# A Mamba layer's scans: the product for the next group issued mid-group, softplus in small steps, and two jobs of later layers moved beside the scans

## The chip, the cores and the metric

The kernel runs on one core of a Trainium2 chip. Its engines are TensorE (PE, with its weight loads as PEld), VectorE (DVE), ScalarE (ACT), GpSimd (POOL) and SyncE (SP), which issues most transfers here. Each engine works through its own queue in order, and semaphores tie the queues together. The metric is the time of one execution on the device in microseconds (us); the lower, the better.

## What is computed

A network of four layers on x of 2 images, 256 channels, 48 x 48 positions (2304 tokens per image), all in float32. Layer 0 is a bidirectional Mamba layer, layer 1 a linear attention with a depthwise convolution and an MLP after a group norm, layer 2 an attention and a mixture of experts that is routed over a graph, layer 3 an attention and a second mixture of experts. What the change touches, cut from the reference:

```python
# layer 0, for each direction s in (f, b)
xs = silu(conv4(xi) + conv_b)                      # 512 inner channels
proj = xs @ xproj_w.T                              # 16 for dt, 16 for B, 16 for C
dt = softplus(proj[..., :16] @ dtproj_w.T + dtproj_b)
def step(h, ...):                                  # h: 512 channels x 16 states
    h = exp(d_t[..., None] * A) * h + (d_t * u_t)[..., None] * B_t[:, None, :]
    return h, einsum('bdn,bn->bd', h, C_t)         # u is xs
y = ys + u * D;  out = seq + ((y_f + y_b) * silu(z)) @ out_proj_w.T

# layer 1 begins with a group norm: 32 groups of 8 channels, one mean and variance
# per group and image over all positions
# layer 2, three heads: e = x @ W_embed[h].T + b_embed[h]; q, k, v are thirds of the
# sequence; the output goes through W_out. The kernel multiplies W_embed[h].T with
# itself and with W_out.T beforehand, so that only 256 x 512 is needed per head.
```

## The kernel before

**Order of the queues.** The kernel is written with a framework that takes the instructions in the order in which the Python code emits them, assigns buffers and semaphores, and then makes each engine's queue itself: an instruction that is ready early in its planning can stand ahead of one that was emitted before it. The order in the code is thus a priority; the order on the chip is read from the trace.

**Layer 0.** Tokens are cut into chunks of W = 384 columns, NCH = 6 per image. `order` lists 24 chunks: image 0 forward, image 0 backward, image 1 forward, image 1 backward. `scan` works through one chunk: 4 blocks of 128 channels (d) times 16 states (n) make 64 scans of 128 x 384, taken in 16 groups of GN = 4 states. A group needs
- `bb` and `cc` (L354, L356): 4 rows each of B and C, broadcast to 128 partitions by a transfer on SP, used by two groups, two buffers each;
- `db` (L359): POOL's product of `dtu` (dt times u) and `bb`, 128 x 1536, two buffers;
- for each state: ACT's exp into PSUM (`hs`, L376, five banks), DVE's scan (L382 forward, L385 backward), the product with C (`hc`, L390: on POOL where `on_pool`, for one or two states of a group, else on DVE), a copy of the last column into `state` (L392, ACT), and a matmul with the identity that adds `hc` into `yp` (L344).

After every second state, a slot, `scan` lets the generators in `beside` go on, in proportion: 32 slots in a chunk. One is `prepare` (L252) for the next chunk, 15 steps by slot 25: convolution on PE, Silu, the projection to dt, B and C, then softplus as max(v, 0) + log(1 + exp(-|v|)) with a correction for the rounding of 1 + exp(-|v|): exp (L302), 1 + exp (L305), log (L307), minus 1 (L308), all on ACT; L310, L311 and L312 on DVE over 128 x 1536; the product `dtu` on POOL (L314). Another is `project_in` (L168), layer norm and input projection of a later chunk, in the first ten chunks; a third `project_out` (L318), which adds a finished backward chunk to the residual `xres` (L328). Outside of `scan`, PSUM results go through one bank (`hold`, tag mm).

**Layer 1** begins with `group_norm(0)` (L510): twelve `bn_stats` on DVE (L517), two tiny matmuls with `gmat`, and the normalization (L533) into `xn`; then L547 multiplies with the weights. Lists of edges for layer 2 are sorted on DVE meanwhile (`sort_list`, `sort_rest`).

**Layer 2** begins with the products of its weights for three heads: loads of `w_eo` (L708, L709), 72 matmuls L713 and 144 matmuls L721 of one column; then transposes (L741) and the first product of the attention, L750, which needs `gm`.

Of the kernel before, what the change touches and what calls it, by code (L numbers as in the profile page):

```python
# [18 lines left out]
F32 = mybir.dt.float32  # L19
# [33 lines left out]
class Env:  # L53
# [20 lines left out]

    def uid(self):
        self.n_pools += 1
        return self.n_pools
# [41 lines left out]

def load_x(E, b, c):  # L120
    xin = E.p["x"].rearrange("b (k p) n -> p b k n", p=P)
    E.nc.sync.dma_start(
        E.xres[:, :, b * L + c * W : b * L + (c + 1) * W], xin[:, b, :, c * W : (c + 1) * W]
    )
# [4 lines left out]
def layer0(ctx, E):  # L129

# [32 lines left out]
    def hold():  # L163

        pool, tag = (ps, "mm") if scanning else (psh, "hs")
        return pool.tile([P, W], F32, tag=tag, name="mm")

    def project_in(b, c):  # L168
# [15 lines left out]
        rs = up.tile([P, W], F32, tag="rs", name="rs")  # L184
# [6 lines left out]
        nc.vector.reciprocal(rs, rs)  # L191
        yield
        nc.vector.tensor_tensor(h, h, bc(rs, [P, 2, W], 1), ALU.mult)
        for k in range(2):
            nc.vector.scalar_tensor_tensor(
                h[:, k, :], h[:, k, :], E.v("ln_g", k, 1), pos[:, k, :], ALU.mult, ALU.add
            )
        yield
# [39 lines left out]
    one = big.tile([P, 2], F32, name="one")  # L238
    nc.vector.memset(one[:, 0:1], 1.0)
    nc.vector.memset(one[:, 1:2], -1.0)  # L240
# [11 lines left out]
    def prepare(b, s, c, got):  # L252
# [52 lines left out]
        nc.scalar.activation(dtu, ex, AF.Identity, bias=one[:, 0:1])  # L305
        yield
        nc.scalar.activation(ln, dtu, AF.Ln)  # L307
        nc.scalar.activation(dtu, dtu, AF.Identity, bias=one[:, 1:2])  # L308
        yield
        nc.vector.tensor_tensor(ex, ex, dtu, ALU.subtract)  # L310
        nc.vector.tensor_tensor(dt, dt, ln, ALU.add)  # L311
        nc.vector.tensor_tensor(dt, dt, ex, ALU.add)  # L312
        yield
        nc.gpsimd.tensor_tensor(dtu, dt, xs, ALU.mult)  # L314
        got.extend((b, s, c, xs, y, dt, dtu, bcd))
        yield
# [14 lines left out]
    def scan(step, beside, b, s, c, xs, y, dt, dtu, bcd):  # L331
# [20 lines left out]
        for d0, g in [(d0, g) for d0 in range(0, DB, 2) for g in range(NS // GN)]:  # L352
            bb = wp.tile([P, GN, W], F32, tag="bb", name="bb")
            nc.sync.dma_start(bb, bcd[16 + g * GN : 16 + (g + 1) * GN, :].partition_broadcast(P))  # L354
            cc = wp.tile([P, GN, W], F32, tag="cc", name="cc")
            nc.sync.dma_start(cc, bcd[32 + g * GN : 32 + (g + 1) * GN, :].partition_broadcast(P))  # L356
            for d in (d0, d0 + 1):
                db = wp.tile([P, GN, W], F32, tag="db", name="db")
                nc.gpsimd.tensor_tensor(db, bc(dtu[:, d, :], [P, GN, W], 1), bb, ALU.mult)  # L359
                if g == 0:  # L360

                    while waiting and waiting[0][1] < d0:
                        add_state(*waiting.pop(0)[1:])
                    yp[d] = psy.tile([P, W], F32, tag=f"y{d % 2}", name=f"yp{d}")
                    nc.tensor.matmul(
                        yp[d], lhsT=w_d[s][:, d, :], rhs=xs[:, d, :], start=True, stop=False
                    )
                    if not fwd:
                        nc.tensor.matmul(
                            yp[d], lhsT=E.ident, rhs=yf[:, d, :], start=False, stop=False  # L370
                        )
                for j in range(GN):
                    n = g * GN + j
                    on_pool = j in GP[(g + d) % 2]
                    hs = psh.tile([P, W], F32, tag="hs", name="hs")
                    nc.scalar.activation(  # L376
                        hs, dt[:, d, :], AF.Exp, scale=nega[s][:, d * NS + n : d * NS + n + 1]
                    )
                    to = wp.tile([P, W], F32, tag="ho", name="ho", bufs=4) if on_pool else hs
                    init = 0.0 if step == 0 else state[:, d, n : n + 1]  # L380
                    if fwd:
                        nc.vector.tensor_tensor_scan(to, hs, db[:, j], init, ALU.mult, ALU.add)  # L382
                        last = to[:, W - 1 : W]
                    else:
                        nc.vector.tensor_tensor_scan(  # L385
                            to[:, ::-1], hs[:, ::-1], db[:, j, ::-1], init, ALU.mult, ALU.add
                        )
                        last = to[:, 0:1]
                    hc = wp.tile([P, W], F32, tag="hcp" if on_pool else "hc", name="hc", bufs=4)
                    (nc.gpsimd if on_pool else nc.vector).tensor_tensor(hc, to, cc[:, j, :], ALU.mult)  # L390
                    if step < NCH - 1:
                        nc.scalar.copy(state[:, d, n : n + 1], last)  # L392
                    while waiting and waiting[0][0] + LAG <= at:
                        add_state(*waiting.pop(0)[1:])
                    if on_pool:
                        waiting.append((at, d, hc))
                    else:
                        add_state(d, hc)
                    at += 1
                    if j % 2:  # L400
                        slot += 1
                        for i, (steps, n_steps, end) in enumerate(beside):
                            while done[i] * end < n_steps * slot and next(steps, beside) is not beside:
                                done[i] += 1
# [4 lines left out]
        for steps, _, _ in beside:  # L409
            for _ in steps:  # L410
                pass

# [7 lines left out]
    for _ in prepare(0, "f", 0, ready):  # L420
        pass
    scanning = True
    pieces = [(0, c) for c in range(2, NCH)] + [(1, c) for c in range(NCH)]
    after = None
    for i, (b, s, step, c) in enumerate(order):
        now, ready = ready, []
        beside = [(after, 2, 5)] if after else []
        if i + 1 < len(order):
            nb, s2, _, c2 = order[i + 1]
            beside.append((prepare(nb, s2, c2, ready), 15, 25))  # L430
        if i < len(pieces):
            beside.append((project_in(*pieces[i]), 12, 32))
        scan(step, beside, *now)
# [26 lines left out]
def layer1(ctx, E, edges):  # L460
# [21 lines left out]
    gmat = big.tile([P, P], F32, name="gmat")  # L482
    same_block(E, lw, gmat, 3, 1.0 / 8)
# [26 lines left out]
    def group_norm(b):  # L510

        xb = E.xres[:, :, b * L : (b + 1) * L]
        mv = wp.tile([P, 2, 2], F32, tag="mv", name="mv")
        for k in range(2):
            st = wp.tile([P, NCH, 6], F32, tag="st", name="st")
            for c in range(NCH):
                nc.vector.bn_stats(st[:, c, :], xb[:, k, c * W : (c + 1) * W])  # L517
            nc.vector.bn_aggr(mv[:, k, :], st)
        pg = ps.tile([P, 2], F32, tag="mm", name="pg")
        nc.tensor.matmul(pg, lhsT=gmat, rhs=mv[:, :, 0], start=True, stop=True)  # L520
        gm = wp.tile([P, 2], F32, tag="gm", name="gm")
        nc.vector.tensor_copy(gm, pg)
        dv = wp.tile([P, 2], F32, tag="dv", name="dv")
        nc.vector.tensor_tensor(dv, mv[:, :, 0], gm, ALU.subtract)
        nc.vector.tensor_tensor(dv, dv, dv, ALU.mult)
        nc.vector.tensor_tensor(dv, dv, mv[:, :, 1], ALU.add)
        gv = ps.tile([P, 2], F32, tag="mm", name="gv")
        nc.tensor.matmul(gv, lhsT=gmat, rhs=dv, start=True, stop=True)
        gr = wp.tile([P, 2], F32, tag="gr", name="gr")
        nc.scalar.activation(gr, gv, AF.Sqrt, bias=E.eps[1e-5])  # L530
        nc.vector.reciprocal(gr, gr)
        for k in range(2):
            nc.vector.tensor_scalar(  # L533
                E.xn[:, k, b * L : (b + 1) * L], xb[:, k, :], gm[:, k : k + 1], gr[:, k : k + 1],
                ALU.subtract, ALU.mult,
# [151 lines left out]
def layer2_attn(ctx, E):  # L687
# [3 lines left out]

    nc, tc, p = E.nc, E.tc, E.p
    NH, D = 3, 768
    S = L // NH
    DT, ST, HW2 = D // P, S // P, S // 2
# [4 lines left out]
    ub = big.tile([P, NH, 4], F32, name="ub")  # L700
    with (
        tc.tile_pool(name="l2wt", bufs=2) as wts,
        tc.tile_pool(name="l2wps", bufs=2, space=PSUM) as ps,
    ):
        for h in range(NH):

            w_eo = wts.tile([P, DT, 2 * C], F32, tag="w_eo", name="w_eo")
            nc.sync.dma_start(w_eo[:, :, 0:C], p["W_embed"][h].rearrange("(k p) m -> p k m", p=P))  # L708
            nc.sync.dma_start(w_eo[:, :, C:], p["W_outT"].rearrange("(k p) m -> p k m", p=P))  # L709
            for m in range(2):  # L710
                pg = ps.tile([P, 2 * C], F32, tag="pg", name="pg")
                for k in range(DT):
                    nc.tensor.matmul(  # L713
                        pg, lhsT=w_eo[:, k, m * P : (m + 1) * P], rhs=w_eo[:, k, :],
# [1230 lines left out]
```

## Time and profile before

| what | value |
|---|---|
| three timed runs | 5452.36, 5459.55, 5462.36 us; median 5459.55 |
| the profiled execution, its own time | 5504.47 us |
| its span | 5502.7 us, 47222 instructions |
| busy, share of the span | PE 87%, PEld 48%, DVE 64%, ACT 43%, POOL 44% |
| mean granted TensorE clock | 0.949 |
| layer 0's scans | 103 to 2391 us |
| layer 2's weight products | 3118 to 3182 us |

The profiled execution is slower than the timed ones by 0.8%; durations come from it. A row of the profile names the engine, the line of kernel.py, the operation, what it writes and reads, the shapes, and in brackets how long the engine had been idle before it and what ended that. A busy share over the whole span mixes stages with different limits, so the stages are read one by one.

### The profile page before, as it was taken

How to read it: one execution, taken by the hardware profiler on the slowest of the kernel's cores; microseconds unless marked ns; L12 is line 12 of the kernel's file. 1: busy time of each engine (PE TensorE's matmuls, PEld its weight loads, DVE VectorE, ACT ScalarE, POOL GpSimd, SP SyncE). 2: the span in 40 equal slices, each digit the busy share in tenths (PEclk: the TensorE clock that was granted, in tenths of full speed). 3: DMA queues.
4: the chain of work that ended last, by engine and by line, in shares of the span. 5: the costliest groups of instructions: out<-in, count | busy, mean ns of one | idle time of the engine just before them, and what ended most of it. 6: DMA issues, size and time to landing. Idle time of an engine off the chain costs nothing. (4 is left out here: it accounts for less than half of the span.)

```text
span 5502.7 us, 47222 instructions
## 1 busy us (share of the span) xinstructions
PE 4797.7 (87%) x15246; PEld 2649.9 (48%) x15246; DVE 3499.6 (64%) x5380; ACT 2371.5 (43%) x4935; POOL 2398.4 (44%) x1295
## 2 busy tenths in 40 slices
PE   7888788888877787879999999998799999998996
PEld 3444344444333343435555555565455555554664
DVE  4899988888999888999994234456534401212333
ACT  5767777666767566622222123322023322222220
POOL 3888887888989888830000000048412100001112
PEclk8999999999999899999999899999899999999997
DMA  4444444443444444421100100111111100001323
GB/s 155 166 171 177 165 178 160 160 157 137 173 150 173 150 161 153 151 100 37 41 26 2 39 1 0 37 38 24 14 58 46 46 6 6 9 6 23 83 76 80
DMA packets 173646, 486.56 MB, mean 88 GB/s; under 512 B 31487, under 2 KB 96516, under 8 KB 173124
## 3 DMA queue, kind: packets, MB, share of 16 engines
q1 hardware_dynamic: 165252, 471.82, 24.3%
q0 software_dynamic: 8128, 11.55, 1.6%
q8 instruction: 124, 2.03, 0.1%
q14 instruction: 142, 1.16, 0.1%
HBM read 416.44 MB, written 66.86 MB: 88 GB/s over the span
## 5 line engine op out<-in xcount | busy, mean ns | idle before, releaser
L344 PE MATMUL yp<-hc,ident 128*128 128x384 f32 x3072 | 1199.9, 523 | 293.7 <-DVE hc L390 253.8
L359 POOL TENSOR_TENSOR db<-dtu,bb 128x1536 f32<-128x1536 f32 x384 | 1333.3, 3473 | 45.5 <-issue 16.5
L344 PEld LDWEIGHTS yp<-hc,ident 128*128 128x128 f32 x3072 | 574.7, 198 | 875.3 <-DVE hc L390 451.3
L390 POOL TENSOR_TENSOR hc<-ho,cc 128x384 f32<-128x384 f32 x576 | 582.6, 1020 | 183.6 <-DVE ho L382 81.9
L390 DVE TENSOR_TENSOR hc<-hs,cc 128x384 f32<-128x384 f32 x960 | 501.3, 544 | 38.9 <-PE yp L344 37.7
L376 ACT ACTIVATE hs<-dt,negab 128x384 f32<-128x384 f32 x768 | 435.2, 582 | 92.6 <-DVE ho L385 41.4
L376 ACT ACTIVATE hs<-dt,negaf 128x384 f32<-128x384 f32 x768 | 434.6, 582 | 58.4 <-DVE hc L390 27.7
L385 DVE TENSOR_TENSOR_SCAN hs<-hs,state,db 128x384 f32<-128x384 f32 x400 | 396.6, 1015 | 55.8 <-POOL db L359 30.3
L382 DVE TENSOR_TENSOR_SCAN hs<-hs,state,db 128x384 f32<-128x384 f32 x400 | 397.1, 1014 | 30.0 <-POOL db L359 23.2
L1770 POOL DMA_INDIRECT xe<-xt_d,token x48 | 52.4, 1091 | 726.4 <-issue 715.0
L266 PE MATMUL mm<-xw,w_cv 128*128 128x384 f32 x768 | 288.8, 512 | 64.5 <-ACT xs L270 26.6
L1704 PE MATMUL po<-at,xtok 128*128 128x384 f32 x864 | 329.7, 506 | 7.7 <-ACT at L1702 7.5
L912 POOL PARTITION_ALL_REDUCE most<-most x1 | 0.4, 382 | 738.8 <-DVE most L911 738.8
L1354 PE MATMUL ph<-xn,w 128*128 128x384 f32 x768 | 292.9, 523 | 28.0 <-issue 10.4
L1695 PE MATMUL sp<-qT,xn 128*128 128x384 f32 x864 | 317.2, 486 | 0.0
L1702 ACT ACTIVATE at<-sp 128x384 f32<-128x384 f32 x216 | 104.9, 491 | 472.5 <-PE sp L1695 472.4
L1358 ACT ACTIVATE hid<-ph,vec 128x384 f32<-128x384 f32 x192 | 110.8, 582 | 338.8 <-PE ph L1354 254.5
L627 PE MATMUL pf<-t,wfc 128*128 128x384 f32 x768 | 255.4, 489 | 0.0
L646 PE MATMUL po<-hid,wfc 128*128 128x384 f32 x768 | 253.6, 486 | 0.0
L385 DVE TENSOR_TENSOR_SCAN ho<-hs,state,db 128x384 f32<-128x384 f32 x240 | 241.2, 1005 | 15.3 <-ACT hs L376 15.1
L382 DVE TENSOR_TENSOR_SCAN ho<-hs,state,db 128x384 f32<-128x384 f32 x240 | 240.3, 1001 | 6.3 <-ACT hs L376 6.2
L266 PEld LDWEIGHTS mm<-xw,w_cv 128*128 128x128 f32 x768 | 146.0, 196 | 192.7 <-ACT xs L270 43.2
(434 smaller groups left out, 7962.9 us busy)
## 6 DMA issues: line engine op xcount, KB each, us to landing
bb<-bcd SPq DMA_DIRECT2D x192, 768.0 KB
cc<-bcd SPq DMA_DIRECT2D x192, 768.0 KB
xw<-xi_d SPq DMA_DIRECT2D x24, 774.0 KB
w<-in_m_w SPq DMA_DIRECT2D x16, 1024.0 KB
y_d<-y SPq DMA_DIRECT2D x32, 384.0 KB
ye<-y_d SPq DMA_DIRECT2D x32, 384.0 KB
xi_d<-xz SPq DMA_DIRECT2D x48, 192.0 KB
z_d<-xz SPq DMA_DIRECT2D x48, 192.0 KB
```

Of the source, the lines that this page charges most:

```text
L266: nc.tensor.matmul(px, lhsT=w_cv[b, s][:, d * 4 + k, :], rhs=xw[:, d, o : o + W], start=k == 0, stop=k == 3,)
L344: nc.tensor.matmul(yp[d], lhsT=E.ident, rhs=hc, start=False, stop=summed[d] == NS)
L359: nc.gpsimd.tensor_tensor(db, bc(dtu[:, d, :], [P, GN, W], 1), bb, ALU.mult)
L376: nc.scalar.activation(hs, dt[:, d, :], AF.Exp, scale=nega[s][:, d * NS + n : d * NS + n + 1])
L382: nc.vector.tensor_tensor_scan(to, hs, db[:, j], init, ALU.mult, ALU.add)
L385: nc.vector.tensor_tensor_scan(to[:, ::-1], hs[:, ::-1], db[:, j, ::-1], init, ALU.mult, ALU.add)
L390: (nc.gpsimd if on_pool else nc.vector).tensor_tensor(hc, to, cc[:, j, :], ALU.mult)
L627: nc.tensor.matmul(pf, lhsT=wfc1[:, k, f * P : (f + 1) * P], rhs=t1[:, k, :], start=k == 0, stop=k == 1,)
L646: nc.tensor.matmul(po[m], lhsT=wfc2[:, f, m * P : (m + 1) * P], rhs=hid[:, i, :], start=f == 0, stop=f == 15,)
L1354: nc.tensor.matmul(ph, lhsT=w1[:, e, k, f * P : (f + 1) * P], rhs=xn[:, k, c * W : (c + 1) * W], start=k == 0, stop=k == 1,)
L1695: nc.tensor.matmul(sp, lhsT=xn[:, k, t0 + i * P : t0 + (i + 1) * P], rhs=qT[:, k, c * W : (c + 1) * W], start=k == 0, stop=k == 1,)
L1704: nc.tensor.matmul(po[m], lhsT=xtok[:, i, m * P : (m + 1) * P], rhs=at, start=i == 0, stop=i == MT - 1,)
```

## The change

- `begin_group` (new) loads `bb` and `cc` where a pair of groups begins and makes `db`. It is called for the next group after the second state of a group (`j == 1`), also for the first group of the next chunk; before, these stood at the head of each group.
- `prepare` has 19 steps by slot 29 instead of 15 by 25. L308 is gone: its minus 1 is folded into a `scalar_tensor_tensor`. After log come two empty steps, then one step per block of 128 channels with three DVE instructions of 384 columns, and `dtu` for that block on POOL a step later.
- `project_in` has its reciprocal and the two products after it by halves, in 14 steps instead of 12.
- `head_products` (new) makes layer 2's weight products beside the scans, in the twelve chunks after the last `project_in`, three steps in each, with half of the inner dimension at a time: loads; three matmuls of 512 columns, which ACT copies for the first half and DVE adds for the second; six matmuls of one column with one or two small DVE instructions. The result goes to DRAM (`gm_d`), and layer 2 loads it in three transfers.
- `group_stats` (new) holds the statistics of `group_norm`. For image 0 it runs beside the second forward chunk of image 1, in 15 steps; for image 1 it runs where it ran.
- PSUM tiles are declared 512 columns wide and used to 384; `gmat` is made at the very start; the normalization of one piece in layer 3 has a pool of its own.

```diff
+def group_stats(E, wp, bank, b):
...
+    for k in range(2):
+        st = wp.tile([P, NCH, 6], F32, tag="st", name="st")
+        for c in range(NCH):
+            nc.vector.bn_stats(st[:, c, :], xb[:, k, c * W : (c + 1) * W])
+            yield
+        nc.vector.bn_aggr(mv[:, k, :], st)
+    pg = bank()
+    nc.tensor.matmul(pg, lhsT=E.gmat, rhs=mv[:, :, 0], start=True, stop=True)
+    nc.vector.tensor_copy(gm, pg)
+    yield
...
     def project_in(b, c):
...
-        nc.vector.reciprocal(rs, rs)
-        yield
-        nc.vector.tensor_tensor(h, h, bc(rs, [P, 2, W], 1), ALU.mult)
         for k in range(2):
+            half = rs[:, k * (W // 2) : (k + 1) * (W // 2)]
+            nc.vector.reciprocal(half, half)
+            yield
+        for k in range(2):
+            nc.vector.tensor_tensor(h[:, k, :], h[:, k, :], rs, ALU.mult)
             nc.vector.scalar_tensor_tensor(
                 h[:, k, :], h[:, k, :], E.v("ln_g", k, 1), pos[:, k, :], ALU.mult, ALU.add
             )
-        yield
+            yield
...
         nc.scalar.activation(ln, dtu, AF.Ln)
-        nc.scalar.activation(dtu, dtu, AF.Identity, bias=one[:, 1:2])
         yield
-        nc.vector.tensor_tensor(ex, ex, dtu, ALU.subtract)
-        nc.vector.tensor_tensor(dt, dt, ln, ALU.add)
-        nc.vector.tensor_tensor(dt, dt, ex, ALU.add)
         yield
-        nc.gpsimd.tensor_tensor(dtu, dt, xs, ALU.mult)
-        got.extend((b, s, c, xs, y, dt, dtu, bcd))
-        yield
+        for d in range(DB + 1):
+            if d:
+                nc.gpsimd.tensor_tensor(
+                    dtu[:, d - 1, :], dt[:, d - 1, :], xs[:, d - 1, :], ALU.mult
+                )
+            if d < DB:
+                nc.vector.scalar_tensor_tensor(
+                    ex[:, d, :], dtu[:, d, :], -1.0, ex[:, d, :], ALU.add, ALU.subtract
+                )
+                nc.vector.tensor_tensor(dt[:, d, :], dt[:, d, :], ln[:, d, :], ALU.add)
+                nc.vector.tensor_tensor(dt[:, d, :], dt[:, d, :], ex[:, d, :], ALU.subtract)
+            else:
+                got.extend((b, s, c, xs, y, dt, dtu, bcd))
+            yield
...
+    def head_products():
+        DT, D = 6, 768
+        for h, m, z in [(h, m, z) for h in range(3) for m in range(2) for z in range(2)]:
+            w_eo = []
+            for k in range(3):
+                rows = slice((z * 3 + k) * P, (z * 3 + k + 1) * P)
+                t = up.tile([P, 2, W], F32, tag=("pos", "h", "sq")[k], name="w_eo")
+                t = t.rearrange("p k w -> p (k w)")[:, : 2 * C]
+                nc.sync.dma_start(t[:, 0:C], p["W_embed"][h, rows, :])
+                nc.sync.dma_start(t[:, C:], p["W_outT"][rows, :])
+                w_eo.append(t)
+            yield
...
+            yield
...
+            yield
+
+    def begin_group(q, b, s, c, xs, y, dt, dtu, bcd):
+        d0, g, d = groups[q]
+        if d == d0:
+            for n, o in (("bb", 16), ("cc", 32)):
+                held[n] = wp.tile([P, GN, W], F32, tag=n, name=n)
+                nc.sync.dma_start(
+                    held[n], bcd[o + g * GN : o + (g + 1) * GN, :].partition_broadcast(P)
+                )
+        db = wp.tile([P, GN, W], F32, tag="db", name="db")
+        nc.gpsimd.tensor_tensor(db, bc(dtu[:, d, :], [P, GN, W], 1), held["bb"], ALU.mult)
+        return db, held["cc"]
...
+                if j == 1:
+                    if q + 1 < len(groups):
+                        begun = begin_group(q + 1, b, s, c, xs, y, dt, dtu, bcd)
+                    elif following:
+                        begun = begin_group(0, *following)
...
-            beside.append((prepare(nb, s2, c2, ready), 15, 25))
+            beside.append((prepare(nb, s2, c2, ready), 19, 29))
         if i < len(pieces):
-            beside.append((project_in(*pieces[i]), 12, 32))
-        scan(step, beside, *now)
+            beside.append((project_in(*pieces[i]), 14, 32))
+        elif i < len(pieces) + 12:
+            beside.append((islice(heads, 3), 3, 32))
+        if (b, s, step) == (1, "f", 1):
+            beside.append((group_stats(E, up, lambda: hold()[:, 0:2], 0), 15, 32))
+        begun = scan(step, beside, begun, ready, *now)
...
+    for h in range(NH):
+        nc.sync.dma_start(gm[:, h], E.gm_d[h].rearrange("m p c -> p m c"))
```

## The prediction

> **What bounds the kernel now.** The execution on the page spans 5502.7 us and took 5504.47; the three timed runs have a median of 5459.55, 0.8% less. I sum against 5504.47 and scale the result by 5459.55/5504.47 = 0.992. No change smaller than 0.2% (11 us) can be told from none. Part 4 of the page covers only the tail of the last layer, so I went by stage: part 2, then a windows table, then waits and timelines of each stretch that the diff touches.
>
> Part 2 of the page, busy tenths in slices of 137.6 us:
> ```profile
> DVE  4899988888999888999994234456534401212333
> ...
> POOL 3888887888989888830000000048412100001112
> ```
> The first seventeen slices are layer 0's scans. DVE and POOL are both near full there and PE has room. The windows table puts numbers on the scans (103 to 2391 us), on the way into layer 1, and on the start of layer 2 (window, length, then busy us of PE, PEld, DVE, ACT, POOL, and the granted clock):
> ```profile
> 103.00:2391.00 2288.00, 1852.43 (x4994) 914.77 (x4994) 2077.37 (x2677) 1554.32 (x3575) 1962.28 (x983) 0.95 0.44 160
> 2399.00:2418.00 19.00, 1.66 (x6) 1.40 (x6) 18.39 (x49) 2.03 (x4) 4.90 (x4) 0.59 0.92 315
> 3118.00:3185.00 67.00, 66.25 (x230) 43.02 (x230) 18.46 (x46) 0.58 (x1) 0.38 (x1) 0.73 0.19 64
> ```
> The scans are 24 chunks of 95.3 us on average; DVE is idle for 211 us of them (8.8 per chunk), POOL for 326. From 3118 to 3185 PE works alone, on layer 2's weight products. What DVE waits for, and the one wait of POOL that matters, 100 to 2392 us (total, times, longest):
> ```profile
> DVE hs L382 <- POOL db L359: 39.4, 35, 6.8
> ...
> DVE hs L385 <- POOL db L359: 35.4, 34, 2.5
> DVE dt L311 <- ACT state L392: 25.0, 13, 3.6
> ...
> DVE dt L311 <- ACT ln L307: 7.0, 5, 3.1
> DVE ex L310 <- ACT dtu L308: 5.1, 8, 1.2
> ```
> ```profile
> POOL dtu L314 <- DVE dt L312: 96.9, 17, 9.9
> ```
> One chunk shows how they hang together (timelines of DVE, then POOL):
> ```profile
> 2184.64 1.76 DVE L311 TENSOR_TENSOR dt<-dt,ln 128x1536 f32<-128x1536 f32 x1 [1.33 <-ACT state L392]
> 2186.31 1.75 DVE L310 TENSOR_TENSOR ex<-ex,dtu 128x1536 f32<-128x1536 f32 x1
> ...
> 2189.15 1.74 DVE L312 TENSOR_TENSOR dt<-dt,ex 128x1536 f32<-128x1536 f32 x1
> ...
> 2198.85 1.93 DVE L385 TENSOR_TENSOR_SCAN hs<-hs,state,db 128x384 f32<-128x384 f32 x2 [2.02 <-POOL db L359]
> ```
> ```profile
> 2191.04 3.44 POOL L314 TENSOR_TENSOR dtu<-dt,xs 128x1536 f32<-128x1536 f32 x1 [7.03 <-DVE dt L312]
> ...
> 2195.38 3.44 POOL L359 TENSOR_TENSOR db<-dtu,bb 128x1536 f32<-128x1536 f32 x1
> ```
> POOL stands 7.03 us at the head of its queue for DVE's softplus; its next db lands late, and the scan waits 2.02 us (and 0.62 at the group after).
>
> **Part 1, db issued at j == 1 of the group before.** POOL's queue already runs a group ahead: at the end of the stage its order is db 2377.93, hc 2381.33, db 2382.28, hc 2385.67, and that last db is for a group whose first scan starts about 2386.3, while the hc after it belongs to the group before. The order out of the program is thus not the order in the queue, and I book nothing for the move itself: same 384 products, same bb and cc loads (two buffers each, issued when a buffer comes free), ahead of the same hc. If it helps where POOL is behind, that is in the next sum.
>
> **Part 2, softplus in small steps.** Per prepared chunk (23 of them inside the scans):
> - *db waits.* The two rows make 74.8 us, of which 12.2 fall in the first chunk, which the change leaves alone: 62.6. In the chunk shown 2.64 of 3.11 come from the 7.03 us stall, 85%. With four dtu products of a quarter width, each issued a step after its dt, the stall should go: -53 (0 to -63).
> - *ACT.* L308 goes (1.58 us). From the exp at 2181.22 to the next scan fed by ACT at 2188.22 DVE did 3.51 us of softplus in a gap that it could not have scanned in. The hole in the exps becomes 6.4 - 1.58 = 4.8 us, but softplus now comes two empty steps later and no longer fills it: 4.8 + 3.5 - 6.4 = +1.9 per chunk at worst (+44), 1.58 less at best (-36). I take the middle, +4.
> - *More instructions.* Three of 1.75 (5.25) become eight TENSOR_TENSOR and four SCALAR_TENSOR_TENSOR of 384 columns. L390 runs in pairs 0.46 apart, L195 0.51: 4 x (0.46 + 0.46 + 0.51) = 5.7, +0.47 per chunk, +11. POOL's 3.43 becomes 4 x 0.97, +0.45, on POOL's own slack (326 us). In project_in one reciprocal of 2.55 becomes two of half the width, one product of 0.95 two of half: nothing within 0.1 each.
> - *Waits between DVE and POOL.* The three instructions read both inputs from SBUF, and such an instruction does not start while POOL works:
> ```profile
> 1523.68 1.92 DVE L310 TENSOR_TENSOR ex<-ex,dtu 128x1536 f32<-128x1536 f32 x1
> ...
> 1525.99 4.51 DVE L312 TENSOR_TENSOR dt<-dt,ex 128x1536 f32<-128x1536 f32 x1
> ```
> ```profile
> 1523.94 4.94 POOL L359 TENSOR_TENSOR db<-dtu,bb 128x1536 f32<-128x1536 f32 x1
> ```
> POOL's db, begun under L310, took 4.94 instead of 3.44, and L312 behind it 4.51 instead of 1.74. Inside the scans L310 to L312 lose 21.6 us over 69 instructions this way, L193 11.8 over 9, L195 0.8 over 22. Today the stall at dtu keeps POOL quiet just when L310 to L312 run; the change takes that cover away and makes four arrivals of one. Ends: no wait (-22), or the 2.77 of the L312 above at every step (4 x 23 x 2.77 - 22 = +233). The first instruction of a step should wait as L310 to L312 and L193 do, (21.6 + 11.8)/78 = 0.43, and the two right behind it as L195, 0.04 each: 0.51 per step. That is 92 x 0.51 - 22 = +25, and +5 for the second step that project_in gets in nine chunks.
>
> The Trainium skill, page "SBUF — State Buffer", section "Who interferes with whom", says that a DVE instruction with two SBUF inputs contends with a GpSimd instruction that reads SBUF, and that whoever issues first holds the shared port for its whole length while the other fully blocks; the 4.51 and 4.94 above agree. Taken alone it speaks against this change: POOL is inside a db 16 x 3.44 of 95.3 us, 58%, so each of twelve instructions would wait 0.58 x 1.72 = 1.0 us, an estimate from that page's rule, and the sum would be 276 - 22 = +254 in place of +25. I go by L195, whose two follow one another directly and hardly wait.
>
> Scans: -53 + 4 + 11 + 30 = -8.
>
> **Part 3, group norm of batch 0.** Before, layer 0's last add ends at 2399.7 and layer 1's first matmul (L547) starts at 2417.61, after twelve bn_stats and two tiny matmuls. After, only the two L533 (1.47 each) remain. POOL's memset of img holds DVE until 2403.8 (a CAST takes 4.24 there), so about 2407: -10.6; layer 1 is then full on DVE (191.5 of 200 us), where at least the 12 x 0.47 removed counts: -9 (-4 to -13).
>
> **Part 4, layer 2's products.** 72 matmuls L713 and 144 L721 leave a PE that has no one beside it. L750 stood at 3185.16. The first 1.57 MB that were loaded there from 3113.23 were used at 3118.3; gm is 1.57 MB, and the transposes L741 need none of it. L750 could start at 3118.5: -66.6. But 18.46 us of DVE work (normalization and sorting, third window) lay under the products and now stand before the copies and maxima of the attention: between -66.6 and -48 I take half, -58.
>
> **What parts 3 and 4 add to the scans.** bn_stats 12 x 0.47 and ten small ones: 7 us on DVE in one chunk. Products: six adds of 128x512 (0.69 for L717), eighteen tiny ones: 6 us over twelve chunks. PE takes 2 to 4 us more per chunk; it waits today for hc, and DVE's four hc buffers hide it. If they do not, another 24. The loads (9.4 MB) lie 16 slices of a chunk ahead, DMA share 0.44; if SP stood behind one, bb and cc would too, and they have a pair of groups in hand. +13 (0 to +37). The rest has one answer, nothing: same_block at the very start lies beside the first loads, the banks of 512 columns are the same banks, and layer 3's separate pool has the same work.
>
> **Sum:** -8 - 9 - 58 + 13 = -62 on 5504.47; x 0.992 = -61.5; 5459.55 - 61.5 = **5398 us**.
>
> **Rivals.**
> *The scans gain what they wait for:* softplus still finds POOL quiet. -63 - 36 + 11 - 11 = -99 for the scans, -153 in all: 5308. For it: a stall of 96.9 us goes. Against: in chunks 13 to 17, where POOL seldom stalls, a chunk takes 86.5 to 91.6 us, and 16 x 3.43 + 24 x 0.97 + 4 x 0.97 + 5.7 = 87.8 is a floor once POOL and those instructions exclude one another.
> *The port wait takes the stall's place (slower):* POOL always has a product in hand, and a step waits as L312 does in chunks 12 to 19 of 0 to 23, 13.4/8 = 1.67. 101 steps x 1.67 - 22 = +147; scans -53 + 4 + 11 + 147 = +109; in all +55: 5514. It decides from (54 + 53 - 4 - 11 + 22)/101 = 1.13 us per step on. For it: that row is of chunks with a busy POOL. Against: 0.31 per instruction over the whole stage.
> *The mid-group issue does nothing and the small steps nothing for db:* POOL goes from waiting for one long dt to waiting for four short ones. db waits 0 instead of -53: -9 in all, 5451.
>
> **How the numbers follow.** Forecast 0.45 (own range 5370 to 5430), faster scans 0.25, port wait 0.15, nothing for db 0.15. Faster by over 0.2%: 0.44 + 0.25 + half of the last 0.07 = 0.76; within 0.2%: 0.08; slower: 0.16. The range leaves out the fast half of the first rival and most of the slow one: 5315 to 5480.
>
> **What would show it.** Right: L713 and L721's successors lie before 2400, the first L750's successor starts within 15 us of the last layer 1 add; the first layer 1 matmul within 9 us of it; POOL's wait for dt under 30 us; the scans' length within 30 of 2288. Wrong: softplus instructions of 384 columns with a mean over 0.9 us (the port), DVE waits for db still at 60, or DVE rows piled up ahead of layer 2's copies.

## The result, and the profile after

The changed kernel took 5515.76 us (median of four runs, 5511.01 to 5521.27) against 5457.56 (5452.36 to 5462.36) of the kernel before, run beside it: ratio 1.0108, 95% interval 1.0096 to 1.012. It is slower by 58 us where 5398 us was forecast. The profiled execution took 5511.01 us, its span is 5509.2.

Part 2 of its page, busy tenths in slices of 137.7 us:
```profile
DVE  5999999999999999999998334446734401212333
...
POOL 3887787778888887882000000018712100001112
```
DVE, which had digits of 8 and 9 in the scans, now has nothing but 9 after the first slice, and for a slice longer. The windows table gives the numbers (scans, the way into layer 1, the start of layer 2; columns as before):
```profile
93.80:2515.60 2421.80, 1952.98 (x5217) 969.12 (x5218) 2280.81 (x2950) 1535.64 (x3562) 1991.99 (x1054) 0.93 0.45 156
2516.00:2531.00 15.00, 7.54 (x21) 3.69 (x20) 13.80 (x24) 1.76 (x3) 5.22 (x3) 0.84 0.53 159
3213.00:3238.00 25.00, 16.19 (x52) 9.17 (x50) 16.82 (x30) 3.87 (x5) 0.00 (x0) 0.83 0.19 63
```
The scans last 2421.8 us instead of 2288.2: +133.6. DVE is busy for 203 us more (2077.4 to 2280.8) and idle for 70 less (211 to 141). The two gaps behind them did shrink: from the last scan to layer 1's first matmul 26.5 to 14.6 us, from layer 1's last matmul (L646, now L738) to the attention's first in layer 2 73.3 to 13.5; in the 25 us that end there DVE now works 16.8 (third row: normalization and sorting, which lay under the products before). The scans also begin 9.1 us earlier. That is 133.6 - 9.1 - 11.9 - 59.7 = +52.9, and +55 with 2.5 that layer 2's attention is longer; +58 was timed. The two profiled executions differ by only 7 us because that of before spent 51 us more in a part that nothing touches, layer 2's experts (846 us from their first matmul to layer 3's first, against 796 here and 799 to 809 in every run below).

What DVE waits for in the scans, and POOL's wait for softplus:
```profile
DVE hc L489 <- PE yp L449: 41.5, 38, 4.3
...
DVE hs L481 <- POOL db L432: 9.9, 17, 1.7
...
DVE hs L484 <- POOL db L432: 7.7, 14, 0.8
```
```profile
POOL dtu L350 <- DVE dt L359: 53.1, 59, 4.3
```
The waits for db are down from 74.8 to 17.6 us, as the change meant; 6.8 of the 74.8 stood before the first scan, so 50 were won between the first scan and the last. The price stands in no list of waits, only in how long instructions take (groups by shape: busy us, mean ns):
```profile
L489 DVE TENSOR_TENSOR hc<-hs,cc 128x384 f32<-128x384 f32 x960 | 501.0, 539 | 43.3 <-PE yp L449 41.5
...
L358 DVE TENSOR_TENSOR dt<-dt,ln 128x384 f32<-128x384 f32 x92 | 128.7, 1403 | 7.0 <-ACT state L491 5.4 <-ACT ln L345 1.5
L359 DVE TENSOR_TENSOR dt<-dt,ex 128x384 f32<-128x384 f32 x94 | 103.6, 1103 | 0.0
L355 DVE SCALAR_TENSOR_TENSOR ex<-dtu,ex 128x384 f32<-128x384 f32 x92 | 90.2, 1003 | 10.9 <-ACT dtu L343 7.7 <-ACT state L491 2.9
L234 DVE SCALAR_TENSOR_TENSOR h<-h,vec,pos 128x384 f32<-128x384 f32 x20 | 33.5, 1680 | 0.0
```
An undisturbed one of L355 to L359 takes 0.53 to 0.55 us. Summing over all 276 what each takes beyond that gives 172 us, 0.62 each; before, 69 wide ones lost 21. In project_in L233 and L234 lose 33 us where 12 were lost. A timeline of DVE, then POOL, shows how:
```profile
1809.60 2.99 DVE L358 TENSOR_TENSOR dt<-dt,ln 128x384 f32<-128x384 f32 x1
1812.52 1.01 DVE L481 TENSOR_TENSOR_SCAN hs<-hs,state,db 128x384 f32<-128x384 f32 x1
1813.44 0.53 DVE L359 TENSOR_TENSOR dt<-dt,ex 128x384 f32<-128x384 f32 x1
...
1815.29 0.52 DVE L355 SCALAR_TENSOR_TENSOR ex<-dtu,ex 128x384 f32<-128x384 f32 x1
1815.73 1.35 DVE L358 TENSOR_TENSOR dt<-dt,ln 128x384 f32<-128x384 f32 x1
1817.01 1.01 DVE L481 TENSOR_TENSOR_SCAN hs<-hs,state,db 128x384 f32<-128x384 f32 x1
1817.93 2.84 DVE L359 TENSOR_TENSOR dt<-dt,ex 128x384 f32<-128x384 f32 x1
```
```profile
1808.75 3.42 POOL L432 TENSOR_TENSOR db<-dtu,bb 128x1536 f32<-128x1536 f32 x1
...
1815.51 1.16 POOL L489 TENSOR_TENSOR hc<-ho,cc 128x384 f32<-128x384 f32 x1 [0.45 <-PE yp L449]
1816.63 3.73 POOL L432 TENSOR_TENSOR db<-dtu,bb 128x1536 f32<-128x1536 f32 x1
```
The L358 at 1809.60 ends 0.42 us after POOL's db, the L359 at 1817.93 0.41 us after the next: each ends only once POOL's instruction has ended. Between them a scan runs at its usual 1.01 us and an hc at 0.54. The second thing to see is the order: the three instructions of a step are not together in DVE's queue. A scan stands between L358 and L359, and in the second step shown (from 1815.29) each of the two meets a POOL product of its own, an hc and a db.

### The profile page after: what moved, and what is told of

It reads as the page before. It is cut to its first block, busy times and chain, and to the rows that moved or that the text cites. A ratio compares the mean times of both kernels' runs of the same rounds, so it can differ in the third digit from the quotient of the medians.

```text
span 5509.2 us, 47592 instructions
## 1 busy us (share of the span) xinstructions
PE 4819.8 (87%) x15246; PEld 2661.5 (48%) x15246; DVE 3694.7 (67%) x5631; ACT 2343.2 (43%) x4915; POOL 2427.3 (44%) x1367
## 5 line engine op out<-in xcount | busy, mean ns | idle before, releaser
L449 PE MATMUL yp<-hc,ident 128*128 128x384 f32 x3072 | 1244.1, 537 | 300.1 <-DVE hc L489 285.9
L449 PEld LDWEIGHTS yp<-hc,ident 128*128 128x128 f32 x3072 | 589.9, 204 | 898.8 <-DVE hc L489 501.2
L489 POOL TENSOR_TENSOR hc<-ho,cc 128x384 f32<-128x384 f32 x576 | 590.4, 1031 | 240.8 <-DVE ho L481 101.4
L489 DVE TENSOR_TENSOR hc<-hs,cc 128x384 f32<-128x384 f32 x960 | 501.0, 539 | 43.3 <-PE yp L449 41.5
L1423 PE MATMUL ph<-xn,w 128*128 128x384 f32 x768 | 285.4, 514 | 17.6 <-ACT hid L1427 6.9
L491 ACT COPY state<-hs 128x1 f32<-128x1 f32 x800 | 120.4, 155 | 399.8 <-DVE hc L489 397.5
L738 PE MATMUL po<-hid,wfc 128*128 128x384 f32 x768 | 253.6, 486 | 0.0
L1774 PEld LDWEIGHTS po<-at,xtok 128*128 128x128 f32 x864 | 150.1, 189 | 176.8 <-ACT at L1772 108.4
```

The source lines that it names most:

```text
L449: nc.tensor.matmul(yp[d], lhsT=E.ident, rhs=hc, start=False, stop=summed[d] == NS)
L738: nc.tensor.matmul(po[m], lhsT=wfc2[:, f, m * P : (m + 1) * P], rhs=hid[:, i, :], start=f == 0, stop=f == 15,)
L1423: nc.tensor.matmul(ph, lhsT=w1[:, e, k, f * P : (f + 1) * P], rhs=xn[:, k, c * W : (c + 1) * W], start=k == 0, stop=k == 1,)
L1774: nc.tensor.matmul(po[m], lhsT=xtok[:, i, m * P : (m + 1) * P], rhs=at, start=i == 0, stop=i == MT - 1,)
```

## Experiments

**Theory P:** the new time is DVE waiting for POOL inside softplus's small instructions, because they are many and POOL is no longer held still. (Below, "the port" is short for this waiting.) **Rivals:** the moved jobs slow the scans (M); the new issue of db, or the sheer number of instructions, does (I). Before's median lies between 5452 and 5458 us throughout; ratios are to before.

| kernel | us | ratio, 95% interval | scans, us |
|---|---|---|---|
| before | 5457.56 | 1 | 2288.2 |
| after | 5515.76 | 1.0108 (1.0096 to 1.012) | 2421.8 |
| e1_moves | 5426.34 | 0.9945 (0.9925 to 0.9964) | 2319.5 |
| e2_split | 5523.32 | 1.0126 (1.0105 to 1.0147) | 2361.6 |
| e3_issue | 5454.07 | 1.0001 (0.9991 to 1.001) | 2285.0 |
| e4_port | 5357.06 | 0.9816 (0.9796 to 0.9836) | 2268.6 |
| e5_two | 5431.39 | 0.9955 (0.9941 to 0.997) | 2339.1 |
| e6_proj | 5488.18 | 1.0061 (1.0044 to 1.0078) | 2390.9 |
| e7_quiet | 5420.57 | 0.9935 (0.9918 to 0.9951) | 2323.8 |
| e8_quarter | 5423.36 | 0.9942 (0.9926 to 0.9959) | 2330.7 |
| b1_fold | 5374.31 | 0.9853 (0.9837 to 0.987) | 2272.5 |
| b2_hc6 | 5353.13 | 0.9815 (0.9799 to 0.9832) | 2246.9 |
| b3_fine | 5368.77 | 0.9841 (0.9825 to 0.9857) | 2272.7 |
| b4_both | 5349.15 | 0.9806 (0.979 to 0.9822) | 2245.3 |

### The change in its parts

**e1_moves.** From the kernel after; `prepare` and `project_in` are those of before, and:
```diff
-            db, cc = begun
+            db, cc = begin_group(q, b, s, c, xs, y, dt, dtu, bcd)
...
-                if j == 1:
-                    if q + 1 < len(groups):
-                        begun = begin_group(q + 1, b, s, c, xs, y, dt, dtu, bcd)
```


> The kernel after with softplus, project_in and the issue of db as in the kernel before: only layer 2's weight products and the group norm of image 0 stay beside the scans. Theory P (softplus's small DVE instructions wait for the port that they share with POOL): the scans lose no more than the 13 us (0 to 37) of the forecast, the two jobs save 12 + 57 us as measured in the changed kernel: 5457 - 56 = 5400 us (5390 to 5425), faster than both kernels. Rival M (the jobs moved in slow the scans): the scans stay over 2350 us long, the time at 5490 to 5515.

5426.34 us, faster than both kernels and a hair above P's range; rival M does not hold. The two gaps closed as in the changed kernel (15.1 and 13.5 us), but the scans grew by 31 us, not 13. DVE's wait for hc has 19 of them:
```profile
DVE hc L480 <- PE yp L440: 56.7, 53, 8.5
```
It was 37.7 before. PE comes late with its sums while it works on the products, and hc's four buffers do not cover that.

**e2_split.** The kernel before with the new end of `prepare` (19 steps by 29), nothing else.

> The kernel before with softplus in small steps and nothing else. Theory P: 276 small DVE instructions at a mean of 1.0 to 1.4 us instead of 0.53; the scans lose some 172 - 22 us to the port, +11 to more instructions, and win back up to 57 of db waits and 20 of waits for ACT: +60 to +110, 5517 to 5567 us. Rival M: what was lost lies in the jobs moved in, so 5400 to 5460 here.

5523.32 us: within P's range, and the scans 73 us longer from softplus alone. Its 276 instructions lose 181 us, at means of 1.14, 1.35 and 1.14 us (L316, L319, L320); the waits for db fall to 21.7.

**e3_issue.** The kernel before with `begin_group` as in the change, nothing else.

> The kernel before with db issued mid-group and nothing else. Theory P: within 0.3% of before (5440 to 5475), since POOL's queue ran a group ahead already. Rival I (the new order of POOL's queue costs the scans): 60 us or more above before, 5515 and up.

5454.07 us, ratio 1.0001. The new issue by itself does nothing; waits for db and scans are as before.

**e6_proj.** The kernel after with one reciprocal, one product of 768 columns and 12 steps in `project_in`.

> The kernel after with project_in's reciprocal and products at full width as in the kernel before, and nothing else undone. Theory P: its waits fall from 33 us (L233 and L234) to the 12 of the kernel before: 5515 - 21 = 5494 us (5480 to 5508). Rival (ten chunks of project_in have slack): 5508 to 5520.

5488.18 us, 28 less than after, for the 21 expected. L230 and L232 (the old L193 and L195) lose 11 us here instead of 33.

### Is it the port, and what makes it wait

**e4_port.** From the kernel after:
```diff
-                nc.vector.scalar_tensor_tensor(ex[:, d, :], dtu[:, d, :], -1.0, ex[:, d, :], ...)
-                nc.vector.tensor_tensor(dt[:, d, :], dt[:, d, :], ln[:, d, :], ALU.add)
-                nc.vector.tensor_tensor(dt[:, d, :], dt[:, d, :], ex[:, d, :], ALU.subtract)
+                nc.vector.bn_stats(ex[:, d, 0:6], dtu[:, d, :])
+                nc.vector.bn_stats(ln[:, d, 0:6], ln[:, d, :])
+                nc.vector.bn_stats(dt[:, d, 0:6], dt[:, d, :])
```


> The kernel after with each of softplus's 276 small DVE instructions (two inputs from SBUF) replaced by a bn_stats of 384 columns, which has one input, in the same place of the queue and with the same chain dt to dtu; the logarithm's part of softplus is left out by that, and the scans' decay is another. A bn_stats beside POOL took 0.538 us in the changed kernel, an undisturbed small instruction about 0.53. Theory P: the rows stay at 0.54 to 0.6 us, the scans lose 172 us of their 2422, and the time is 5335 to 5375 us. Rival I (the number and the place of the instructions, or the order of the queues, cost it): 5490 to 5520, as after.

5357.06 us, 159 less than after, in P's range. The groups:
```profile
L356 DVE BATCH_NORM_STATS2 ln<-ln 128x6 f32<-128x384 f32 x92 | 50.0, 550 | 12.1 <-ACT state L489 9.8 <-ACT ln L345 2.2
L355 DVE BATCH_NORM_STATS2 ex<-dtu 128x6 f32<-128x384 f32 x92 | 49.0, 551 | 8.9 <-ACT dtu L343 7.8 <-ACT state L489 1.1
L357 DVE BATCH_NORM_STATS2 dt<-dt 128x6 f32<-128x384 f32 x92 | 48.1, 547 | 0.1
```
As many instructions, as many columns, the same chain from dt to dtu, and all at 0.55 us with nothing lost. So the number and the place of the instructions cost nothing by themselves. A bn_stats differs in a second way, it writes 6 columns and not 384. That this is not the reason is seen in the changed kernel's hc on DVE (L489, first row of the groups above): it writes 384 columns to SBUF, but reads one input from PSUM, and its 960 took 0.56 us at most although POOL was at work when 770 of them began. What costs is that both inputs are read from SBUF.

**e5_two.** From the kernel after: softplus over two blocks at a time, `dtu` too (`two = slice(d, d + 2)`, d = 0 and 2), with an empty step behind each.

> The kernel after with softplus in two steps of 768 columns (6 DVE instructions per chunk) in place of four of 384 (12), in the same span of steps. Theory P1 (each instruction waits for what is left of the POOL instruction in progress, 0.62 us on average whatever its own width: 172 us over 276 instructions): 138 instructions wait 86 us, so 5515 - 86 = 5430 us (5405 to 5460). Rival P2 (the wait goes with the columns that are worked on): the sum of the waits stays near 172 us, the time at 5505 to 5525.

5431.39 us. The means are 1771, 2014 and 1248 ns against 0.94 us undisturbed; 138 instructions lose 100 us, 0.72 each, where 276 half as wide lost 0.62 each. What is paid is a wait per instruction, nearly whatever its width, so P1 holds. Even the sums of one column in `head_products` pay it: six of them (`ub`, both inputs in SBUF) took 2.83 us on average in e4_port, against 0.15 for an undisturbed one in e7_quiet.

**e7_quiet.** From the kernel after; all twelve in one step, then the one wide `dtu`:
```diff
+        for d in range(DB):
+            nc.vector.scalar_tensor_tensor(ex[:, d, :], dtu[:, d, :], -1.0, ex[:, d, :], ...)
+            nc.vector.tensor_tensor(dt[:, d, :], dt[:, d, :], ln[:, d, :], ALU.add)
+            nc.vector.tensor_tensor(dt[:, d, :], dt[:, d, :], ex[:, d, :], ALU.subtract)
+        yield
+        nc.gpsimd.tensor_tensor(dtu, dt, xs, ALU.mult)
```


> The kernel after with the same twelve small softplus instructions per chunk, but all in one step, followed by one dtu of 1536 columns on POOL, where the kernel before had them (15 steps by slot 25). Theory C (what kept the waits low before was not the width but that POOL stood at the head of its queue for the one dtu, quiet while DVE did softplus): the twelve instructions wait 15 to 60 us in sum in place of 172, the waits for db come back (+40 to +57), in all 5410 to 5470 us. Rival N (twelve instructions give POOL twelve chances to get in between, wherever they stand): waits of 150 us or more, 5515 to 5570 us.

5420.57 us, in theory C's range:
```profile
L348 DVE SCALAR_TENSOR_TENSOR ex<-dtu,ex 128x384 f32<-128x384 f32 x92 | 64.8, 751 | 7.4 <-ACT dtu L343 3.8 <-ACT state L485 3.4
L351 DVE TENSOR_TENSOR dt<-dt,ln 128x384 f32<-128x384 f32 x92 | 57.3, 654 | 10.5 <-ACT state L485 7.9 <-ACT ln L345 2.6
L352 DVE TENSOR_TENSOR dt<-dt,ex 128x384 f32<-128x384 f32 x92 | 50.9, 585 | 0.0
```
The twelve per chunk lose 31 us instead of 172; the waits for db come back by 26 us (17.6 to 43.3), less than the 40 to 57 expected. What each instruction stands behind, and whether POOL was at work when it started, read from the trace:

| kernel | directly behind one of softplus: count, lost per instruction | others: count, lost per instruction | POOL free at the start |
|---|---|---|---|
| before | 9, 0.00 us | 60, 0.35 us | 51 of 69 |
| after | 74, 0.41 us | 202, 0.70 us | 127 of 276 |
| e7_quiet | 228, 0.00 us | 48, 0.62 us | 249 of 276 |
| e8_quarter | 229, 0.15 us | 47, 0.66 us | 192 of 276 |

**e8_quarter.** e7_quiet with `dtu` in four parts, which tells whether standing together protects or POOL's being idle:

> e7_quiet with its one dtu of 1536 columns as four of 384, one per block, still in the step after the twelve DVE instructions. In e7_quiet 228 of the 276 instructions stand directly behind another one of softplus and lose 0.8 us in sum; POOL is free at the start of 227 of them. Theory C (they lose nothing because POOL has nothing to do, not because they stand together): each dtu can now start once its block's dt is done, so POOL works while DVE is at the next block; an instruction behind another one that met a POOL product of 384 columns took 1.31 us instead of 0.55 in the changed kernel, so three per chunk: 3 x 23 x 0.8 = +55 us of waits, 31 to some 85 us; on the other side db's waits fall by up to 20 us: 5430 to 5475 us. Rival A (instructions that stand together keep the port): the waits stay under 45 us, the time at 5395 to 5425 us.

5423.36 us: by the time alone this is rival A's range, near its upper end, and below theory C's. The waits are not A's, which were to stay under 45 us: those that stand together lose 33 us instead of 0.8, and 50 of them found a `dtu` in progress and took 1.22 us; the 178 that found POOL free took 0.55. Standing together does not protect; an idle POOL does. In all 64 us are lost, 33 more than in e7_quiet and within the 31 to 85 expected, and the waits for db fall by 17 (43.3 to 26.2). The scans are 7 us longer and the time is the same within noise, so theory C's time was wrong and its mechanism is read from the rows.

### A faster kernel

**b1_fold.** From e1_moves, L308 folded into a wide instruction:
```diff
-        nc.scalar.activation(dtu, dtu, AF.Identity, bias=one[:, 1:2])
...
-        nc.vector.tensor_tensor(ex, ex, dtu, ALU.subtract)
+        nc.vector.scalar_tensor_tensor(ex, dtu, -1.0, ex, ALU.add, ALU.subtract)
```


> e1_moves (layer 2's products and the group norm moved, all else as before) with the minus 1 of L308 folded into a scalar_tensor_tensor of 1536 columns, so that ACT has one instruction of 1.58 us less per chunk; softplus stays three wide instructions and one dtu. Theory P: the port waits stay at 12 to 25 us; if ACT's hole is on the path, up to 23 x 1.58 = 36 us are won: 5390 to 5426 us. Rival (ACT's hole is hidden): 5420 to 5432.

5374.31 us, 52 less than e1_moves: more than expected, 2.3 us per chunk for an ACT instruction of 1.58. The port waits stay at 20 us. In the scans, 47 us shorter, DVE's waits that ACT ends fall from 100 to 72 us; its wait for hc falls too, from 56.7 to 39.2, and why is not shown.

**b2_hc6.** `bufs=4 if on_pool else 6` for hc, `bufs=1` for pr and xz.

> b1_fold with six buffers instead of four for DVE's product hc (the room comes from one buffer each for pr and xz). What it tells: whether the jobs that were moved in cost the scans 31 us (2288 to 2320 in e1_moves) because PE, busy with their matmuls, returns hc's buffers late. Theory Q (PE in bursts): DVE's wait for hc falls from 40 us to under 15, time 5374 - 25 to - 40 = 5335 to 5350 us. Rival (the wait moves on to the next late thing, exp from ACT or db from POOL): 5360 to 5380 us.

5353.13 us, 21 less: between the two.
```profile
DVE hc L478 <- PE yp L438: 22.2, 24, 2.7
```
The wait for hc falls from 39.2 to 22.2, most of what was won, and does not vanish. That PE returns hc's buffers late holds; that this was all of the 31 us is not shown.

**b3_fine.** b1_fold with the products by halves of 256 columns (`w_eo[k][:, i * C : (i + 1) * C]`), four steps per set.

> b1_fold with each set of three product matmuls of 512 columns cut into two of 256, a step apart (four steps per set in place of three; six more small DVE or ACT instructions). Theory Q: shorter bursts on PE, DVE's wait for hc in the twelve chunks falls by 5 to 15 us, 5360 to 5370 us. Rival (the burst's length does not matter, more instructions do): 5372 to 5385 us.

5368.77 us, in theory Q's range but only 5.5 less, with intervals that overlap b1_fold's; DVE's wait for hc did not fall (43 us). Nothing follows for the burst's length.

**b4_both.**

> b2_hc6 and b3_fine together. Theory Q: with six buffers the bursts are covered already, so b2_hc6's time to within 5 us: 5335 to 5350 us. Rival: 5355 to 5385 us.

5349.15 us, ratio 0.9806 (0.979 to 0.9822): the fastest here, though not to be told from b2_hc6. Against the kernel after it is 167 us.

## Why the prediction was wrong, step by step

**The step that failed: the waits between DVE and POOL, booked at +25 and +5.** They measured 172 - 21 = +151 in softplus and +21 in project_in. Per step of three, 1.87 us instead of 0.51. Both prices in it were wrong.
- *"the two right behind it as L195, 0.04 each."* There were hardly any: for POOL I had read that the order out of the program is not the order in the queue; for DVE I took the three of a step to stay together. In the changed kernel 202 of 276 stand behind a scan or an hc. And the price held only while POOL was idle: instructions behind one another lost 0.004 in e7_quiet, 0.15 in e8_quarter and 0.41 in the changed kernel. The rows of before had both. In eight of the nine steps of project_in inside the scans, L195's pair (18 instructions in all, not 22) stands behind a scan or an hc, not behind L193. No POOL product held 17 of the 18 up; the whole 0.8 us is the one that met an hc of POOL, directly behind another L195, and took 1.43 of the 1.96 us in the last DVE row here (DVE, then POOL):
```profile
217.03 2.72 DVE L193 TENSOR_TENSOR h<-h,rs 128x768 f32<-128x768 f32 x1
219.68 1.01 DVE L382 TENSOR_TENSOR_SCAN hs<-hs,state,db 128x384 f32<-128x384 f32 x1
220.60 1.12 DVE L195 SCALAR_TENSOR_TENSOR h<-h,vec,pos 128x384 f32<-128x384 f32 x2
...
809.82 1.96 DVE L195 SCALAR_TENSOR_TENSOR h<-h,vec,pos 128x384 f32<-128x384 f32 x2
```
```profile
810.37 1.00 POOL L390 TENSOR_TENSOR hc<-ho,cc 128x384 f32<-128x384 f32 x1 [3.23 <-PE yp L344]
```
- *"the first instruction of a step should wait ... 0.43."* That price came from instructions under the cover which the change takes away, as the same paragraph says. Before, POOL was free at the start of 51 of 69, in the changed kernel of 127 of 276, and the price rose to 0.70.

The forecast's 92 x 0.51 is 47 us, the measured term 172. With all 276 at the old 0.43 it would have been 119; with the forecast's neighbours at the new prices, 92 x 0.70 + 184 x 0.41 = 140. Each error alone makes most of the miss, and which one weighs more depends on the order in which they are put right.

**The rival that held** is the port wait in the stall's place, forecast at 5514 us with a chance of 0.15 and measured at 5515.76. Its row, L312 among chunks with a busy POOL, gave 1.67 us per step; 1.87 came, beyond the 1.13 from which it decides. That row was nearer than the average over the stage: it showed what happens where POOL is not stalled, which the change was to bring about everywhere. That its time fits to within 2 us is partly luck: its scans, +122 with the moved jobs, were 12 us short of +133.6, and the rest of the kernel gained 11 us more than its -67.

**The Trainium skill's rule** (page "SBUF — State Buffer", section "Who interferes with whom") agrees with e4_port, where one input in place of two took the waits away. The estimate made from it, +254 with every instruction waiting 1.0 us, was 103 us above the measured +151, as mine was 126 below: 0.62 was measured. A db was in progress at the start of 73 of the 276, 26%, not of 58%; 76 more met a shorter POOL product, an hc or a dtu.

**What held.** db waits outside the first chunk: -53 forecast, -48 measured (62.6 to 14.4). Layer 2's products: -58, measured -60 in the gap and +2.5 in the attention behind it. Group norm: -9, measured -12. The issue of db: nothing, e3_issue within 0.1%. Not foreseen was that the first chunk gains too: its first db no longer waits for the whole of softplus, the 6.8 us before the first scan are gone and the scans begin 9.1 us earlier (6.2 in e2_split).

**What was mis-sized beside it.** The moved jobs in the scans: +13, measured +31 where they stand alone (e1_moves); the case named, that hc's four buffers do not cover PE, came true there, with 19 us. In the changed kernel the wait for hc rose by only 4 (37.7 to 41.5). ACT: +4 within -36 to +44; waits of DVE that ACT ends fell by 24 us (99 to 76). All this is small beside the port.

**The sum again** for the scans, from DVE's rows between the first scan and the last, each instruction counted to the start of the next. Instructions: softplus +165.5 (151 of it the port, the rest twelve in place of three, booked at 11), project_in +22.8 (21 of it the port), the moved jobs +17.8. Waits: for db -50.4, for ACT -23.6, for PE +6.5. Everything else: -5.0. Together +133.6.

## What to carry to other kernels

Cutting a DVE instruction with two SBUF inputs into pieces beside a busy GpSimd multiplies its waits, since each piece waits for the GpSimd instruction in progress; keep such pieces wide, or put them where GpSimd has to wait anyway. A stall on one engine may be the cover of another: before removing it, price the covered instructions from the stretch where the stall does not occur, not from the average. And read in the trace what a new instruction will stand behind in its queue; what the program emits together may not stay together.

## What the runs showed of the hardware that was not expected

- Waits for the port appear in no list of waits: 172 us stood as longer instructions only (1.0 to 1.4 us on average, undisturbed 0.53 to 0.55).
- A bn_stats (one SBUF input, 384 columns) lost nothing beside POOL: in e4_port all 276 took 0.53 to 0.57 us, though POOL was at work when 225 of them began; a scalar_tensor_tensor of the same width lost up to 3.2 us in the changed kernel.
- Two-input instructions that follow one another do not keep POOL out: in e8_quarter 50 of 229 found a POOL product begun in between and took 1.22 us instead of 0.55.
- A profiled execution can carry time in a part that no one touched: layer 2's experts took 846 us in that of before and 796 to 809 in the thirteen others. The cause is open.
